# Moving the attention's transposes to the front of the full-array block in a windowed-attention and Fourier kernel

## The chip, the cores and the metric

The kernel runs on one core of one Trainium2 chip. The metric is the device time of one launch in microseconds (us); lower is better. The core has a matrix engine (PE, with its weight loads listed apart as PEld), a vector engine (DVE), a scalar engine (ACT), GpSimd (POOL) and a queue that only issues DMAs here (SP). All arithmetic is in float32.

## The reference, cut to what matters

The input is 32 images of 56 x 56 tokens with 128 channels. Two residual layers follow each other:

```
x = x + attention(groupnorm(x))      # 7x7 windows, shifted by 3, 4 heads of 32
x = x + ff(fourier(groupnorm(x)))    # DCT along each axis, 32 modes, mix, inverse DCT
                                     # ff: relu(h @ W1 + b1) @ W2 + b2, 512 hidden
```

Each group normalization is over 4 channels and the whole image, so an image's second layer starts only when all of its attention is done. The attention is `softmax(q k' + bias + mask) v`, then a projection with bias.

## The kernel before, in words

Nothing goes to another core and each image is loaded once. The attention works by rows of windows: an image has 8 rows (`NWR`) of 8 windows. One *cycle* starts one row; the loop at the end of the function runs over 8 x 32 cycles and a tail. In a cycle the PE does, for different rows and images, these pieces, which the text names by letters:

- **Q**: the products for queries and keys of row `cycle` (`attn_qk`, lines 363 and 370, one matmul each of 392 columns). ACT writes q (line 366) and half of k (line 375), DVE the other half of k (line 383).
- **S**: the scores of row `cycle` (`attn_scores`, line 417). DVE adds the bias (line 425). `attn_max` takes the maximum on DVE (435) and subtracts it on POOL (436). `attn_exp` is one ACT instruction (442). One cycle later `attn_divide` sums on DVE (447), takes the reciprocal (449) and multiplies on POOL (450).
- **W**: the values of row `cycle` (`attn_v`, line 395, ACT copy on line 402).
- **T**: the transposes of the finished attention matrix (`attn_transpose`, line 461, 8 matmuls; copies by DVE on 471 and ACT on 469).
- **V**: attention times values, row `cycle - 2` (`attn_values`, line 486, 64 small matmuls). ACT and DVE move the result to `oT` (lines 519, 517).
- **P**: the projection of that row (`attn_project`, line 528). DVE adds it to the image (536), SP writes the rows to `scr` in DRAM (542).
- **G**: two rows of the next image are transposed and copied to `xw` by ACT (`image_groups`, line 262; copies on 274, 275, 280; statistics on DVE, line 284). Its bias addition on POOL is `image_bias` (line 293). `image_norm` turns the statistics into scaled weights: a chain of small DVE instructions (lines 320 to 338), one POOL power (342), an ACT multiplication (349), `nb` on DVE (346) and a matmul N (line 352).
- The Fourier layer of earlier images: `transform` (637), `mix` (671; ACT copies `z`, SP writes `zscr`), `load_modes` (SP reads `zT`, line 692), `modes_back` **B** (710), `ff_in` **F** (753, 8 matmul records for one group of tokens, ACT relu on 761, POOL addition of `b2` on 743) and `ff_out` **O** (773, DVE addition on 785, SP output on 797 to 805).

The pieces use the array in different shapes: Q, T, P, G, F and O take all of it, W, `transform` and `mix` 128 x 64 of it, S and B 64 x 64, V 32-column tiles. A cycle runs through them in the order `full_first` (full array), `half_columns`, `quarters`, `eighths`, `full_last` (full array), so `full_last` and the next `full_first` form one block.

The order on PE, ACT, DVE and POOL is the order in which the program is written (`manual_schedule` names these four engines). The order of the DMAs on SP is left to the framework's own planner.

The Fourier work of the image in its *phase* c = (cycle - 10) mod 8 is spread by c: phase 0 `transform` along the width, 1 and 2 along the height, 3 `mix` (height), 4 and 5 `mix` (width), 4 to 7 B (two groups each). The feed-forward part is cut in 7 groups of tokens by `FF_GROUPS`; `FF_AT` says at which c, counted on to 14, each one runs. So a group runs in phases 7, 0, 1, 2, 4, 5 and 6, and phase 3 has none. G runs at the end of phases 1, 2, 3 and 4, the norm of the next image in phase 5. Cycles 0 to 9 (`first_rows`) have attention alone.

PSUM is cut in two pools of four banks that are handed out in turn: `pa` for the attention, `pc` for the Fourier layer. A matmul that takes a bank waits until the copy out of the bank's last use is done.

Of the kernel before, what the change touches and what calls it, by code (L numbers as in the profile page):

```python
# [23 lines left out]
WT = WS * WS  # L24
# [14 lines left out]
HALVES = (slice(0, P // 2), slice(P // 2, P))  # L39
SQRT_S = float(np.sqrt(float(S)))  # L40
QS = HD ** (-0.5)
FF_GROUPS = (HB, HB, HB, HB, HB, 320, 256)
FF_AT = (7, 8, 9, 10, 12, 13, 14)
PW = JP + WT
CONV_BEGIN = NWR + 2
# [3 lines left out]
def swin_fourier_kernel(  # L49
# [194 lines left out]
    def image_begin(b):  # L244
        im = Image()
        im.b = b
        im.x = xls.pop(b) if b in xls else load_image(b)
        im.xw = {}
        im.st = small.tile([P, NWR, 6], F32, tag="st0", name="st0", bufs=2)
        im.part = small.tile([TC, 2, C // 4, NWR], F32, tag="part", name="part", bufs=1)  # L250
        im.scr = dram.tile([S, S, C], F32, tag="scr", name="scr", bufs=2)
        return im

    def image_groups(im, i):


        pt = [attn_bank(), attn_bank()]
        pts = [
            p[:, : n * S].rearrange("p (j r s) -> p j r s", r=n, s=WS) for p, n in zip(pt, (8, 6))
        ]  # L260
        for c in range(7):
            nc.tensor.transpose(  # L262
                pts[c // 4][:, :, 2 * (c % 4) : 2 * (c % 4) + 2],
                im.x[:, WS * i // 2 + c],
                ident_x[:, :, SS:].rearrange("p r (j s) -> p j r s", s=WS),
            )
        for k in range(2):

            im.xw[i + k] = big.tile([P, RT + JP - WT], F32, tag="xw", name="xw", bufs=10)
            nc.gpsimd.memset(im.xw[i + k][:, RT:], 0.0)  # L270
            xw = im.xw[i + k][:, :RT]
            dst = xw.rearrange("p (j r s) -> p j r s", r=WS, s=WS)
            if k:
                nc.scalar.copy(dst[:, :, 0], pts[0][:, :, WS])
                nc.scalar.copy(
                    dst[:, :, 1:].rearrange("p j r s -> p j (r s)"),
                    pts[1].rearrange("p j r s -> p j (r s)"),
                )
            else:
                nc.scalar.copy(  # L280
                    dst.rearrange("p j r s -> p j (r s)"),
                    pts[0][:, :, :WS].rearrange("p j r s -> p j (r s)"),
                )
            nc.vector.bn_stats(im.st[:, i + k], xw)
        if im.b:
            image_bias(im, i)

    def image_bias(im, i):

        n0, n1 = WS * i // 2, WS * (i + 2) // 2  # L290
        for a, e in ((n0, n0 + 4), (n0 + 4, n1)):
            piece = im.x[:, a:e]
            nc.gpsimd.tensor_tensor(  # L293
                piece, piece, bproj.unsqueeze(1).to_broadcast([TC, e - a, C]), ALU.add
            )
# [158 lines left out]
    def attn_transpose(im, i, r):  # L454

        a = a_sb[r % 3]
        im.aT = []
        for hf in range(2):
            pt = attn_bank()
            for h in range(NH):  # L460
                nc.tensor.transpose(  # L461
                    pt[:PW, h * P : h * P + PW],
                    a[:PW, h, 2 * hf : 2 * hf + 2].rearrange("p w j -> p (w j)")[:, :PW],
                    ident[:PW, :PW],
                )
            aT = work.tile([P, 4, P], F32, tag="aT", name="aT")
            src = pt[:PW].rearrange("p (m x) -> p m x", x=P)[:, :, :PW]
            if hf:
                nc.scalar.copy(aT[:PW, :, :PW], src)  # L469
            else:  # L470
                nc.vector.tensor_copy(aT[:PW, :, :PW], src)
            im.aT.append(aT)

    def attn_values(im, i, r):


        v = v_sb[r % 3]
        po = [attn_bank(), attn_bank()]
        HALF = RT // 2
        po4 = [p[:, :HALF].rearrange("p (r n s) -> p n r s", r=WS, s=WS) for p in po]  # L480
        for f in range(2):
            for e in range(2):
                for h in range(NH):
                    for u in range(2):
                        ks = slice(u * JP, u * JP + WT)
                        nc.tensor.matmul(  # L486
                            po4[u][h * HD : (h + 1) * HD, 2 * f + e],
                            lhsT=v[ks, 2 * f + e, h * HD : (h + 1) * HD],
                            rhs=im.aT[f][ks, h, e * JP : e * JP + WT],
                            start=True,  # L490
                            stop=True,
                        )

        if i % 2 == 0:
            im.oT = work.tile([P, 2 * RT], F32, tag="oT", name="oT")
        oT = im.oT


        oTr = oT[:, i % 2 * RT : (i % 2 + 1) * RT].rearrange("p (r x) -> p r x", x=S)
        for u in range(2):  # L500
            src = po[u][:, :HALF].rearrange("p (r f x) -> p r f x", r=WS, f=2)
            x0 = SS + u * 2 * WS
            if not u:
                dst = bass.AP(
                    oTr.tensor, oTr[:, :, x0:].offset, [oTr.ap[0], [S, WS], [4 * WS, 2], [1, 2 * WS]]
                )
                parts = [(dst, src)]
            else:
                n = S - 4 * WS - x0
                parts = [  # L510
                    (oTr[:, :, x0 : x0 + 2 * WS], src[:, :, 0]),
                    (oTr[:, :, S - n : S], src[:, :, 1, :n]),
                    (oTr[:, :, 0:SS], src[:, :, 1, n:]),
                ]
            for d, f in parts:
                if u:
                    nc.vector.tensor_scalar(d, f, im.bias[:, 2:3], None, ALU.add)  # L517
                else:
                    nc.scalar.activation(d, f, AF.Identity, bias=im.bias[:, 2:3])
# [310 lines left out]
        return []  # L830

    def full_first(cycle, norm):
        im, i = row(cycle - 2)
        if im:
            attn_transpose(im, i, cycle - 2)
        last, j = row(cycle - 3)
        if last:
            sums = attn_sums(last, j)
            next(sums)
        im, i = row(cycle)  # L840
        if im:
            attn_qk(im, i, False)
        for im, c in fourier(cycle):
            for width, g in back_groups(c):
                load_modes(im, width, g)
        next(norm)
        if last:
            next(sums)
        for im, c in fourier(cycle):
            if c == 0:  # L850
                im.stats = fourier_stats(im)
                im.cols = {}
                next(im.stats)
                load_columns(im, 0)
                load_columns(im, 1)
        for im, c in fourier(cycle):
            if c in FF_AT:
                ff_in(im, FF_AT.index(c))
        for im, c in fourier(cycle):
            if c == 0:  # L860
                next(im.stats)
        if row(cycle - 1)[0]:
            attn_divide(cycle - 1)
# [29 lines left out]
    def eighths(cycle):  # L893
        im, i = row(cycle - 2)
        if im:
            attn_values(im, i, cycle - 2)

    def last_out(cycle):
        for im, c in fourier(cycle):
            if c in FF_AT:  # L900
                ff_out(im, FF_AT.index(c))

    def full_last(cycle, norm):
        next(norm)
        if row(cycle - 2)[0]:
            last_out(cycle)
        next_image(cycle)
        if row(cycle)[0]:
            attn_exp(cycle)
        im, j = row(cycle - 2)  # L910
        if im:
            attn_project(im, j)
        next(norm)

    def next_image(cycle):
# [9 lines left out]
    def first_rows(cycle, norm):  # L925
        im, i = row(cycle)
        if im:
            attn_qk(im, i, True)
        if cycle:
            attn_exp(cycle - 1)  # L930
        last, j = row(cycle - 3)
        if last:
            attn_project(last, j)
        im2, i2 = row(cycle - 2)
        if im2:
            attn_transpose(im2, i2, cycle - 2)
        if cycle:
            attn_divide(cycle - 1)
        if im:
            attn_scores(im, i, cycle)  # L940
            attn_max(cycle)
        if im2:
            attn_values(im2, i2, cycle - 2)
        next(norm)
        if last:
            for _ in attn_sums(last, j):
                pass
        if im:
            attn_v(im, i, cycle)
        if cycle < NWR // 2:  # L950
            image_bias(im, 2 * cycle)
        next(norm)
        next_image(cycle)
        if cycle == CONV_BEGIN - 1:
            attn_exp(cycle)
            attn_project(im2, i2)
        next(norm)

    def nothing():
# [100 lines left out]
```

## Time and profile before

| | |
|---|---|
| median of 4 runs | 3686.62 us (3685.34 to 3689.6) |
| the profiled execution, its own time | 3687.07 us |
| its span, first to last instruction | 3685.3 us |
| mean granted PE clock | 0.997 |
| PE busy | 3611.7 us, 61184 matmuls |
| DVE, ACT, POOL busy | 2213.6, 2144.9, 1372.5 us |
| DMA | 388.92 MB, mean 106 GB/s |

The rows of the timeline have the start in us from the span's beginning, the busy time, the engine, the line, what is written from what, and in brackets the idle time just before the instruction with what ended it. Matmuls overlap each other, so a block's length is best taken from its start to the start of the next block. The times of single steps below come from one image in the middle of the profiled execution, around 1560 to 1680 us; the other images repeat it.

### The profile page before, as it was taken

The numbers are of one execution on the slowest core, as the hardware profiler recorded it, in microseconds if no ns is written. First come the engines' busy times: TensorE is split into PE (matmuls) and PEld (weight loads), VectorE is DVE, ScalarE is ACT, GpSimd is POOL, SyncE is SP. The second block draws the span as 40 slices with busy tenths as digits, with TensorE's granted clock in tenths as the row PEclk, the third lists the DMA queues.
The fourth block names the chain that finished last, engine by engine and source line by source line (L and its number), as shares of the span: only waits on it lengthen the run. The fifth ranks groups of instructions, "written<-read, shape, count | busy, mean of one in ns | idle before, by whom it ended". The sixth has DMA issues, their size and how long they took to land.

```text
span 3685.3 us, 139865 instructions
## 1 busy us (share of the span) xinstructions
PE 3611.7 (98%) x61184; PEld 2940.1 (80%) x61184; DVE 2213.6 (60%) x4739; ACT 2144.9 (58%) x4043; POOL 1372.5 (37%) x1421
## 2 busy tenths in 40 slices
PE   7899999999999999999999999999999999999999
PEld 5687888888878888888788887878887888888777
DVE  7756566556665566665666665666656666656641
ACT  5565555655565655566555556555665565565553
POOL 5343334333333333343333343333343333433321
PEclk9999999999999999999999999999999999999999
DMA  4344443443433344334434344443344343433333
GB/s 115 97 106 109 105 110 91 119 106 104 113 96 107 107 110 109 104 96 112 110 101 114 97 110 107 106 113 96 104 107 113 102 114 96 112 107 104 96 102 96
DMA packets 687266, 388.92 MB, mean 106 GB/s; under 512 B 39967, under 2 KB 657600, under 8 KB 686400
## 3 DMA queue, kind: packets, MB, share of 16 engines
q1 hardware_dynamic: 686045, 379.65, 38.0%
q8 instruction: 482, 7.90, 0.9%
q14 instruction: 128, 1.05, 0.1%
q10 hardware_dynamic: 611, 0.32, 0.0%
HBM read 218.29 MB, written 161.48 MB: 103 GB/s over the span
## 4 chain that ended last, share of the span: by engine, by line
PE 91%; DMA 3%; DVE 3%; ACT 1%; issue 1%; POOL 0%; SPq 0%; POOLq 0%; DVEq 0%; ACTq 0%
PE pc L773 20%; PE pc L753 17%; PE pa L395 7%; PE pc L671 6%; PE pc L637 6%; PE pa L528 6%; PE pa L461 5%; PE pa L417 5%; PE pa L363 5%; PE pa L486 4%; PE pc L710 4%; PE pa L370 4%; DMA zT<-zscr 3%; PE pa L262 2%; DVE a L425 1%
## 5 line engine op out<-in xcount | busy, mean ns | idle before, releaser
L773 PE MATMUL pc<-wff,hid 128*128 128x128 f32 x6400 | 779.9, 279 | 1.0 <-ACT hid L761 0.9
L450 POOL TENSOR_TENSOR a<-a,rs 128x784 f32<-128x784 f32 x256 | 389.4, 1521 | 977.9 <-DVE rs L449 872.2
L773 PEld LDWEIGHTS pc<-wff,hid 128*128 128x128 f32 x6400 | 731.8, 190 | 23.5 <-issue 2.6
L753 PE MATMUL pc<-xf,wff 128*128 128x512 f32 (+2 forms) x1792 | 710.7, 539 | 0.9 <-DVE xf L721 0.7
L753 PEld LDWEIGHTS pc<-xf,wff 128*128 128x128 f32 x1792 | 339.3, 190 | 310.1 <-issue 228.8
L761 ACT ACTIVATE hid<-pc,b1sb 128x512 f32<-128x512 f32 (+2 forms) x896 | 532.7, 636 | 87.8 <-PE pc L753 84.0
L436 POOL TENSOR_TENSOR a<-a,mx 128x784 f32<-128x784 f32 x256 | 389.1, 1520 | 453.0 <-DVE mx L435 442.9
L785 DVE TENSOR_TENSOR res<-pc,res 128x512 f32<-128x512 f32 (+3 forms) x257 | 144.0, 571 | 615.1 <-issue 324.8
L293 POOL TENSOR_TENSOR xl<-xl,bproj 112x512 f32<-112x512 f32 (+1 forms) x256 | 286.3, 1141 | 376.1 <-PE pa L262 376.1
L425 DVE TENSOR_TENSOR a<-pa,bm 128x392 f32<-128x392 f32 x512 | 259.7, 550 | 193.4 <-PE pa L417 193.4
L442 ACT ACTIVATE a<-a 128x784 f32<-128x784 f32 x256 | 225.1, 879 | 210.3 <-POOL a L436 210.0
L383 DVE TENSOR_SCALAR k<-pa,heads,bqkv 128x392 f32<-128x392 f32 x246 | 168.5, 685 | 287.6 <-ACT k L375 287.6
L469 ACT COPY aT<-pa 113x452 f32<-113x452 f32 x256 | 137.0, 535 | 301.8 <-PE pa L461 296.8
L402 ACT COPY v<-pa 128x512 f32<-128x512 f32 x256 | 152.6, 596 | 271.0 <-PE pa L395 270.9
L517 DVE TENSOR_SCALAR oT<-pa,bqkv 128x98 f32<-128x98 f32 (+2 forms) x768 | 170.6, 277 | 226.0 <-PE pa L486 226.0
L743 POOL TENSOR_TENSOR res<-res,b2sb 128x512 f32<-128x512 f32 (+2 forms) x256 | 264.0, 1036 | 96.3 <-DMA res<-scr 96.3
L417 PEld LDWEIGHTS pa<-k,q 64*64 64x64 f32 x8192 | 183.5, 132 | 133.9 <-DVE rs L449 68.2
L395 PE MATMUL pa<-wn,xw 128*64 128x128 f32 x4096 | 281.9, 280 | 5.8 <-DVE a L425 3.4
L395 PEld LDWEIGHTS pa<-wn,xw 128*64 128x64 f32 x4096 | 219.8, 137 | 55.9 <-issue 16.4
L528 PE MATMUL pa<-wproj,oT 128*112 128x128 f32 x1792 | 244.2, 276 | 13.9 <-DVE oT L517 7.2
L280 ACT COPY xw<-pa 128x392 f32<-128x392 f32 x128 | 62.1, 485 | 325.9 <-PE pa L262 323.1
L435 DVE TENSOR_REDUCE mx<-a 128x16 f32<-128x784 f32 x256 | 247.1, 965 | 5.5
(91 smaller groups left out, 6071.2 us busy)
## 6 DMA issues: line engine op xcount, KB each, us to landing
zscr<-z SPq DMA_DIRECT2D x512, 112.0 KB
htok<-scr SPq DMA_DIRECT2D x256, 196.0 KB
zT<-zscr SPq DMA_DIRECT2D x192, 256.0 KB
res<-scr SPq DMA_DIRECT2D x160, 256.0 KB
out_dram<-res SPq DMA_DIRECT2D x160, 256.0 KB
scr<-xl SPq DMA_DIRECT2D x128, 224.0 KB
xl<-in_x_dram SPq DMA_DIRECT2D x32, 784.0 KB
xl<-in_x_dram SPq DMA_DIRECT2D x32, 672.0 KB
```

The lines of the kernel that those rows point to most:

```text
L293: nc.gpsimd.tensor_tensor(piece, piece, bproj.unsqueeze(1).to_broadcast([TC, e - a, C]), ALU.add)
L395: nc.tensor.matmul(pv[hs, j * C : (j + 1) * C], lhsT=im.xw[i][:, w * WT : w * WT + JP], rhs=im.w[:, 2 * C : 3 * C], start=True, stop=True,)
L417: nc.tensor.matmul(ps[hp][HALVES[e], pr * 2 * WT : (pr + 1) * 2 * WT], lhsT=q[cs, w * WT : w * WT + JP], rhs=k_sb[cs, :, w], start=True, s ...
L425: nc.vector.tensor_tensor(a[:, 2 * hp : 2 * hp + 2, :, 0:WT].rearrange("p u w j -> p w u j"), ps[hp][:, :RT].rearrange("p (w u j) -> p w u ...
L435: nc.vector.tensor_reduce(mx, a3, axis=AX.X, op=ALU.max)
L436: nc.gpsimd.tensor_tensor(a3, a3, mx.unsqueeze(2).to_broadcast([P, 2 * NWR, WT]), ALU.subtract)
L450: nc.gpsimd.tensor_tensor(a3, a3, rs.unsqueeze(2).to_broadcast([P, 2 * NWR, WT]), ALU.mult)
L528: nc.tensor.matmul(pp[:TC, (n - n0) * C : (n - n0 + 1) * C], lhsT=oT[:, (n - base) * TC : (n - base + 1) * TC], rhs=wproj, start=True, sto ...
L743: nc.gpsimd.tensor_tensor(res[:m, c0:c1], res[:m, c0:c1], b2sb[:m].unsqueeze(1).to_broadcast([m, c1 - c0, C]), ALU.add,)
L753: nc.tensor.matmul(ph[:, :n], lhsT=wff1[:, f * P : (f + 1) * P], rhs=xff[:, t0 : t0 + n], start=True, stop=True,)
L761: nc.scalar.activation(hf[:, :n], ph[:, :n], AF.Relu, bias=b1sb[:, f : f + 1])
L773: nc.tensor.matmul(pf[:m, c * C : (c + 1) * C], lhsT=im.hid[f][:, c * P : c * P + m], rhs=wff2[:, f], start=(f == 0), stop=(f == NF - 1),)
```

## The change

It has six parts.

1. T of a row moves from the start of `full_first` of one cycle to the start of `full_last` of the cycle before, ahead of O. The new function `transpose_next` issues it. Since two rows' transposes now exist at a time, `im.aT` becomes a dictionary by row.
2. In `full_last` P moves ahead of G and of the exponential. The order there was: norm step, O, G, exponential, P, norm step. It is now: T, norm step, O, P, G, exponential, norm step.
3. The seven groups of `FF_GROUPS` are reordered: the 320 and 256 tokens move from places six and seven to places five and six, and a group of 512 comes last. In phases: phase 4 has 320 instead of 512, phase 5 has 256 instead of 320, phase 6 has 512 instead of 256.
4. `image_bias` is merged into `image_groups`, so that image 0 gets its bias there too and not in cycles 0 to 3.
5. In `first_rows` the first step of the next image's norm moves from behind V to the place behind the exponential of the row before. It has an effect in cycle 7 alone.
6. At the end of cycle 9, T of row 8 is issued behind P, where `full_first` of cycle 10 issued it.

```diff
-FF_GROUPS = (HB, HB, HB, HB, HB, 320, 256)
+FF_GROUPS = (HB, HB, HB, HB, 320, 256, HB)
...
             nc.vector.bn_stats(im.st[:, i + k], xw)
-        if im.b:
-            image_bias(im, i)
-
-    def image_bias(im, i):
 
         n0, n1 = WS * i // 2, WS * (i + 2) // 2
...
     def full_first(cycle, norm):
-        im, i = row(cycle - 2)
-        if im:
-            attn_transpose(im, i, cycle - 2)
         last, j = row(cycle - 3)
...
+    def transpose_next(cycle):
+
+
+        im, i = row(cycle - 1)
+        if im:
+            attn_transpose(im, i, cycle - 1)
+
...
     def full_last(cycle, norm):
+        transpose_next(cycle)
         next(norm)
-        if row(cycle - 2)[0]:
+        im, j = row(cycle - 2)
+        if im:
             last_out(cycle)
+            attn_project(im, j)
         next_image(cycle)
         if row(cycle)[0]:
             attn_exp(cycle)
-        im, j = row(cycle - 2)
-        if im:
-            attn_project(im, j)
         next(norm)
...
         if cycle:
             attn_exp(cycle - 1)
+        next(norm)
         last, j = row(cycle - 3)
...
         if im2:
             attn_values(im2, i2, cycle - 2)
-        next(norm)
         if last:
...
-        if cycle < NWR // 2:
-            image_bias(im, 2 * cycle)
         next(norm)
         next_image(cycle)
         if cycle == CONV_BEGIN - 1:
             attn_exp(cycle)
             attn_project(im2, i2)
+            transpose_next(cycle)
         next(norm)
```

More of the change, by code (lines that the diff above doesn't have):

```diff
@@ L247, in image_begin @@
         im.x = xls.pop(b) if b in xls else load_image(b)
-        im.xw = {}
+        im.xw, im.aT = {}, {}
         im.st = small.tile([P, NWR, 6], F32, tag="st0", name="st0", bufs=2)
@@ L456, in attn_transpose @@
         a = a_sb[r % 3]
-        im.aT = []
+        im.aT[i] = []
         for hf in range(2):
@@ L471, in attn_transpose @@
                 nc.vector.tensor_copy(aT[:PW, :, :PW], src)
-            im.aT.append(aT)
+            im.aT[i].append(aT)
     def attn_values(im, i, r):
@@ L488, in attn_values @@
                             lhsT=v[ks, 2 * f + e, h * HD : (h + 1) * HD],
-                            rhs=im.aT[f][ks, h, e * JP : e * JP + WT],
+                            rhs=im.aT[i][f][ks, h, e * JP : e * JP + WT],
                             start=True,
```

## The prediction

> **What bounds the kernel now.** I read the page first, then the waits of PE, then the timeline of one image (1560 to 1680 us), which repeats every 112.8 us.
>
> ```profile
> PE 3611.7 (98%) x61184; PEld 2940.1 (80%) x61184; DVE 2213.6 (60%) x4739; ACT 2144.9 (58%) x4043; POOL 1372.5 (37%) x1421
> PE 91%; DMA 3%; DVE 3%; ACT 1%; issue 1%; POOL 0%; SPq 0%; POOLq 0%; DVEq 0%; ACTq 0%
> ```
>
> PE sets the end. No other engine is near full, so only what PE waits for, or executes more slowly, counts. The change removes no arithmetic. The waits of PE:
>
> ```profile
> PE pc L710 <- DMA zT<-zscr: 10.7, 24, 1.4
> PE pa L352 <- DVE nb L346: 9.3, 2, 4.7
> PE pa L528 <- DVE oT L517: 7.2, 5, 2.3
> PE pa L461 <- POOL a L450: 0.3, 1, 0.3
> ```
>
> They are small, and the modelled ends of matmuls hide some. I therefore took block lengths from start to start and compared equal blocks: over images 2 to 31 the excess above the shortest is 13.2 us at B of phase 6, 15.3 us at G of phase 3 (some 12 of it waiting for `oT`) and 6 us around N. That is what can be won, besides what a new order costs. The fourth line shows that T hardly ever waits for its matrix where it stands.
>
> Phase 3, the one without O:
>
> ```profile
> 1601.15 0.81 PE L486 MATMUL pa<-aT,v 49*32 49x49 f32 x64
> 1601.89 0.98 PE L262 MATMUL pa<-ident_x,xl 112*128 112x112 f32 x7
> 1602.21 0.66 DVE L517 TENSOR_SCALAR oT<-pa,bqkv 128x98 f32<-128x98 f32 x3
> 1603.02 1.10 PE L528 MATMUL pa<-wproj,oT 128*112 128x128 f32 x8
> 1605.44 0.87 ACT L442 ACTIVATE a<-a 128x784 f32<-128x784 f32 x1 [1.95 <-POOL a L436]
> ```
>
> G takes 1.13 us to P's start, against 0.72 elsewhere (1619.18 to 1619.89): P waits for `oT`, 0.15 us behind its DVE row's end. The exponential is here 3.5 us later than G.
>
> From phase 4 to 5:
>
> ```profile
> 1619.18 0.88 PE L262 MATMUL pa<-ident_x,xl 112*128 112x112 f32 x7
> 1619.79 0.48 ACT L280 COPY xw<-pa 128x392 f32<-128x392 f32 x1 [3.75 <-PE pa L262]
> 1620.60 0.89 ACT L442 ACTIVATE a<-a 128x784 f32<-128x784 f32 x1
> 1621.34 0.84 PE L363 MATMUL pa<-xw,wn 128*128 128x392 f32 x2
> 1623.65 0.69 DVE L383 TENSOR_SCALAR k<-pa,heads,bqkv 128x392 f32<-128x392 f32 x1 [0.85 <-ACT k L375]
> 1624.92 0.90 PE L417 MATMUL pa<-k,q 64*64 64x98 f32 x32
> 1628.49 1.52 POOL L450 TENSOR_TENSOR a<-a,rs 128x784 f32<-128x784 f32 x1
> 1629.67 0.81 PE L486 MATMUL pa<-aT,v 49*32 49x49 f32 x64
> ```
>
> ACT makes G's copies and the exponential before it can write q and k. P and T stand between G and Q and hide this. The division ends at 1630.01, only 0.40 us before V's end (1630.41), where T will stand.
>
> Phase 6:
>
> ```profile
> 1636.19 0.48 SPq L692 DMA_DIRECT2D zT<-zscr  x1
> 1636.81 1.89 PE L753 MATMUL pc<-xf,wff 128*128 128x256 f32 x8
> 1638.79 0.90 PE L417 MATMUL pa<-k,q 64*64 64x98 f32 x32
> 1640.77 1.00 PE L710 MATMUL pc<-idctw,zT 64*64 64x112 f32 x32 [0.31 <-DMA zT<-zscr]
> ```
>
> F of 256 tokens ends before k is written (S starts 0.06 us after DVE's k), and B's second half waits for a load issued 4.6 us earlier.
>
> **The change part by part**, per image in the steady state.
>
> *(a) T between V and O.* O's 32 matmuls take 3.68 us behind V (1655.40 to 1659.08) at 0.112 us each, 0.10 more than 32 of them. P's 8 take 0.93 behind the wait after G in phase 3, 0.87 behind O: 0.06 more. No block behind another full-array block shows such an extra. With T first I expect 0.06 there and nothing at O: 0.04 won in each of seven phases, 0.28 (bounds 0 and 0.7). The Trainium skill (TensorEngine Tiling (Array Packing), Key Properties) says that a change of the tiling mode drains the engine, whoever comes next; by that the switch is only moved, and the sum would be 8 us smaller. T's eight matmuls and two copies are otherwise the same, and T's banks are free: they were last used by S's second half and W, whose ACT copy ends at V's end in phase 6 (1643.42), 0.4 us before T's fifth matmul.
>
> *(b) Phase 3.* V 0.74 and T 0.86 reach 1602.75, P still starts at 1603.02, then P 0.93 and G 0.72 with Q at 1604.67, against 1604.74: 0.07 won. DVE's T copy runs behind the maximum, to 1604.30; G's second bank needs it at 1604.35. No gain from here is safe, but none is lost.
>
> *(c) Phase 4, 320 instead of 512.* F takes 2.25 instead of 3.53, so what waits behind it has 1.28 less cover. The exponential waits for POOL as before (1605.44); without T's copy, q starts at 1606.23 and DVE's k ends at 1608.10. S is due at 1608.25: free by 0.1. `zT` landed at 1607.8 and 1608.55 (issue at 1604.97 and 1605.40), needed at 1609.0 and 1609.8: covered. I take 0; bound 0.3.
>
> *(d) Phase 5, 256 instead of 320, Q directly behind G.* With Q's start as 0: G starts at -0.71, its first copy is 0.61 later, the exponential 1.42 later (0.71), q 0.78 behind that (1605.44 to 1606.22) at 1.49, k on ACT at 1.97, DVE's k 0.71 behind and done at 3.36, S possible at 3.42. PE gets there at 1.33 + 1.83 = 3.16: wait 0.26. V then ends at 3.42 + 0.73 + 1.26 + 0.92 + 1.85 + 0.74 = 8.92. The division ends 6.36 behind the start of DVE's k (1623.65 to 1630.01): 9.04, T at about 9.1. Lost: 0.26 + 0.15 = 0.41 (bounds 0.1 and 0.9). Queued behind T on PE are O, P and N; on ACT and DVE, T's copies stand before `wn` and `nb`, which N needs only 2.6 us later. In phases 2 and 3 the same ACT delay of 0.4 us is covered: S comes at Q + 4.9 and 5.9, T has 2.7 and 1.3 us to spare. T in phases 0, 1, 4, 6, 7: 1.2 us or more.
>
> *(e) Phase 6, 512 instead of 256.* S's wait goes: 1.98 against the 1.83 that 8 x 0.216 + 0.10 gives, 0.15. For B: behind P the path to B's second half gets 1.55 us longer by F and 0.9 shorter by T, and P itself comes 0.36 earlier after V. The load, issued behind P's write on SP, has some 0.7 us more; the wait was 13.2 / 29 = 0.45 a piece, 0.9 at most. Won: 0.6 (bounds 0.2 and 0.7). T behind N paid 0.11, Q behind N probably half: 0.07 won.
>
> Sum: -0.28 - 0.07 + 0 + 0.41 - 0.60 - 0.07 = -0.61 us an image, 30 times: **-18.3 us**.
>
> *(f) Once.* First image, where no O fills phases: W waited 0.65, 0.83, 0.62 and 0.78 us for a bank that T's late ACT copy held (now G's, copied first), and P waited 1.1 to 2.3 us behind V in three cycles, of which T fills 0.86 each: -5.5. Last image's phase 3: -0.9. Cycle 7's norm: its DVE chain (2.6 us) now runs ahead of the row's DVE work, but `nb` stays behind the sums in DVE's order; only DVE's idle 0.35 us goes: -0.4. PE's idle time there falls from 4.6 to some 2.3 us. After 4.6 us the 392-column matmuls ran at 0.80 instead of 0.43 us apart, 2.2 us lost in that cycle; after 2.90 us idle (at 103.67) the next blocks were slow too; after 1.06 us (113.81) not. I take no gain; bound -2.2. The Trainium skill (TensorE: Matmul & The Clock Gate, What's actually happening) puts the idle window at about 3.4 us; by that the 2.2 us would be won, though the 2.90 us row disagrees. Image 0's bias: four pairs of 2.24 us on POOL end near 17.3 us instead of inside cycles 0 to 3, where they delayed nothing; the power at 17.08 slips 0.3 us at most, hidden by the bias table, which lets the first scores through only at 27.5. Tail: phase 4's shorter F uncovers `zT` (it waited 0.46 already), and four output chunks instead of two end the kernel: +1.3. Together **-5.4 us** (bounds -10 and +2).
>
> From the profiled execution: 3687.07 - 18.3 - 5.4 = 3663.4. It lay 0.45 above the median: **3663**.
>
> **Rivals.** *Slower: ACT's exponential becomes the bound.* Moved between G's copies and Q, it is on the path to S in phases 4 and 5, exactly where F was shortened, and DVE's k delays the division for T. Against it: the rows above give 0 and 0.41. For it: margins of 0.1 us. Each 0.1 us that q, k and the division come later than computed costs up to 0.3 us an image (S in 4, S and T in 5), so the change turns at 0.25 us; at 0.4 us it is -23.7 + 36 = +12, 3699. *No change*: SP's order is the planner's. If the load in phase 6 stays as late as it is and (a) gives nothing, -0.61 + 0.45 + 0.28 = +0.12 us an image; 30 times that and -5.4 make -1.8, 3685. *More*: with k in time in phase 5 and 0.1 at each O, -0.61 - 0.41 - 0.42 = -1.44 us an image, 3638.
>
> **Numbers.** Forecast case 0.62 (its own range 3648 to 3678), more 0.05, no change 0.13, slower 0.20. The range runs from 3646 to 3697: some 0.05 below, 0.13 above. 0.2% or 7 us is what a measurement of this kernel can tell from no change: faster 0.67, same 0.13, slower 0.20.
>
> **What would show it.** Right: no DMA wait at B in phase 6, O at 3.58 us, W in cycles 11 to 14 without wait. Also S in phase 5 waiting some 0.3 us for DVE's k, and a POOL wait at T in phase 5. Wrong: S of phase 4 or 5 waiting a microsecond, `zT` late in phase 4, or O still 3.68 behind T.

## The result and the profile after

The kernel after takes 3682.87 us (median of 42 runs) where the kernel before takes 3687.66 (63 runs): a ratio of 0.9987 with the interval 0.9982 to 0.9991. That is 4.8 us, or 0.13%: inside what the prediction called no difference, and 20 us short of the forecast. The profiled execution took 3683.4 us with a span of 3681.6; the one before took 3687.07.

PE is busy for 3607.4 us, 98% of the span (3611.7 and 98% before). From the page, the chain that ended last:

```profile
PE 85%; DVE 5%; DMA 4%; ACT 2%; POOL 2%; issue 1%; SPq 1%; ACTq 0%; POOLq 0%; DVEq 0%
```

PE still sets the end, but its share of the chain fell from 91% to 85%, and DVE, POOL, DMA and ACT gained most of what it lost: more of the steps are now released by another engine. The waits of PE (engine, tile, line, what ended the wait: us in total, times, longest) say which:

```profile
PE pc L706 <- DMA zT<-zscr: 8.1, 19, 1.2
...
PE pa L413 <- DVE k L379: 7.3, 32, 0.8
...
PE pa L457 <- POOL a L446: 3.3, 3, 2.4
...
PE pa L524 <- DVE oT L513: 2.0, 2, 1.0
```

Lines are four lower than before. P's wait for `oT` (L524) fell from 7.2 to 2.0 us. B's wait for `zT` (L706) is still 8.1 of 10.7 us, S waits for DVE's half of k (L413) 32 times instead of once, and T now waits for the division (L446).

The modelled ends of matmuls hide part of such waits, so the accounts below go by block starts. I took the time from a block's start to the next one's, in the mean over images 2 to 31. An image took 112.92 us before and takes 112.84 now: 0.08 us less, where 0.61 was forecast. By phase:

| phase | before | after | what moved |
|---|---|---|---|
| 0 | 16.28 | 16.34 | "issue" stalls: transform 3.58 to 3.40, V 0.79 to 1.04 |
| 1, 2, 7 | 44.07 | 44.02 | T and O only |
| 3 | 10.44 | 10.34 | P no longer waits for `oT` behind G |
| 4 to 6 | 42.14 | 42.13 | next two views |

The three phases with the new group sizes are compared as a sum, since the same work stands in other phases. They stayed equal because two waits went and three came. Phase 4 (after, the timeline of all engines):

```profile
1602.91 0.38 SPq L688 DMA_DIRECT2D zT<-zscr  x1
...
1603.39 0.45 SPq L538 DMA_DIRECT2D scr<-xl  x1
...
1603.89 5.25 SPq L688 DMA_DIRECT2D zT<-zscr  x3
...
1606.67 2.04 PE L706 MATMUL pc<-idcth,zT 64*64 64x112 f32 x64
```

The same place before:

```profile
1604.97 0.93 SPq L692 DMA_DIRECT2D zT<-zscr  x2
1606.01 0.44 SPq L542 DMA_DIRECT2D scr<-xl  x1
```

SP now issues the write of the attention row (`scr<-xl`) between the two reads of `zT` that B of phase 4 needs. Before, both reads went out first (1604.97 and 1605.40). Both orders are the same in every image counted. Measured from the start of Q, the second read goes out at 1.52 us instead of 0.66, and its last packet lands at 5.20. F of 320 tokens lets B's second half get there at about the same time, so B takes 2.01 us in the mean instead of 1.64.

Phase 4 to 5 (after, the same view):

```profile
1617.29 0.48 ACT L280 COPY xw<-pa 128x392 f32<-128x392 f32 x1 [3.47 <-PE pa L262]
...
1618.10 0.89 ACT L438 ACTIVATE a<-a 128x784 f32<-128x784 f32 x1
...
1618.72 1.89 PE L749 MATMUL pc<-xf,wff 128*128 128x256 f32 x8
...
1620.07 0.69 DVE L379 TENSOR_SCALAR k<-pa,heads,bqkv 128x392 f32<-128x392 f32 x1 [0.77 <-ACT k L371]
...
1620.81 0.90 PE L413 MATMUL pa<-k,q 64*64 64x98 f32 x32 [0.20 <-DVE k L379]
...
1624.90 1.52 POOL L446 TENSOR_TENSOR a<-a,rs 128x784 f32<-128x784 f32 x1 [0.45 <-DVE rs L445]
...
1626.48 0.87 PEld L457 LDWEIGHTS pa<-ident,a 113*113 113x113 f32 x8 [0.24 <-POOL a L446]
```

ACT copies G, then runs the exponential, then writes q and k. DVE's half of k ends at 1620.76 and S starts 0.05 us later. At the end of the row the division ends at 1626.42 and T starts 0.06 later. F of 256 tokens takes 2.08 us to S's start instead of 1.83, V 0.92 instead of 0.74.

Phase 6 (after, the timeline of PE):

```profile
1635.83 1.71 PE L706 MATMUL pc<-idctw,zT 64*64 64x112 f32 x64
1637.47 1.09 PE L391 MATMUL pa<-wn,xw 128*64 128x128 f32 x16
...
1639.58 1.05 PE L457 MATMUL pa<-ident,a 113*113 113x113 f32 x8
1640.46 3.75 PE L769 MATMUL pc<-wff,hid 128*128 128x128 f32 x32
1644.05 0.82 PE L524 MATMUL pa<-wproj,oT 128*112 128x128 f32 x6
```

B runs through in 1.64 us: the wait for `zT` is gone here. And T to O to P: T takes 0.88 and O 3.59. Before, O behind V took 3.68 and T behind P 0.79. The sum is the same to 0.01 us.

### The profile page after: what moved, and what is told of

It reads as the page before. It is cut to its first block, busy times and chain, and to the rows that moved or that the text cites. A ratio compares the mean times of both kernels' runs of the same rounds, so it can differ in the third digit from the quotient of the medians.

```text
span 3681.6 us, 139841 instructions
## 1 busy us (share of the span) xinstructions
PE 3607.4 (98%) x61184; PEld 2941.7 (80%) x61184; DVE 2226.6 (60%) x4741; ACT 2126.3 (58%) x4043; POOL 1372.0 (37%) x1421
## 4 chain that ended last, share of the span: by engine, by line
PE 85%; DVE 5%; DMA 4%; ACT 2%; POOL 2%; issue 1%; SPq 1%; ACTq 0%; POOLq 0%; DVEq 0%
PE pc L769 19%; PE pc L749 16%; PE pa L457 6%; PE pa L391 6%; PE pc L633 6%; PE pa L524 5%; PE pa L413 4%; PE pa L359 4%; PE pa L482 4%; PE pa L366 4%; PE pc L667 4%; PE pc L706 3%; PE pa L262 2%; DMA zT<-zscr 2%; DMA zscr<-z 1%; POOL a L446 1%
## 5 line engine op out<-in xcount | busy, mean ns | idle before, releaser
L769 PE MATMUL pc<-wff,hid 128*128 128x128 f32 (+1 forms) x6400 | 760.6, 276 | 1.0 <-ACT hid L757 0.8
L769 PEld LDWEIGHTS pc<-wff,hid 128*128 128x128 f32 (+1 forms) x6400 | 732.4, 190 | 10.0 <-issue 2.9
L446 POOL TENSOR_TENSOR a<-a,rs 128x784 f32<-128x784 f32 x256 | 389.4, 1521 | 912.2 <-DVE rs L445 885.0
L362 ACT ACTIVATE q<-pa,bqkv 128x392 f32<-128x392 f32 x256 | 150.2, 587 | 285.4 <-PE pa L359 283.7
L739 POOL TENSOR_TENSOR res<-res,b2sb 128x512 f32<-128x512 f32 (+2 forms) x256 | 263.7, 1035 | 99.3 <-DMA res<-scr 99.3
L413 PEld LDWEIGHTS pa<-k,q 64*64 64x64 f32 x8192 | 183.4, 132 | 139.7 <-DVE rs L445 45.5
L457 PE MATMUL pa<-ident,a 113*113 113x113 f32 x2048 | 267.8, 274 | 7.8 <-POOL a L446 3.3
```

Of the source, the lines that this page charges most:

```text
L413: nc.tensor.matmul(ps[hp][HALVES[e], pr * 2 * WT : (pr + 1) * 2 * WT], lhsT=q[cs, w * WT : w * WT + JP], rhs=k_sb[cs, :, w], start=True, s ...
L446: nc.gpsimd.tensor_tensor(a3, a3, rs.unsqueeze(2).to_broadcast([P, 2 * NWR, WT]), ALU.mult)
L457: nc.tensor.transpose(pt[:PW, h * P : h * P + PW], a[:PW, h, 2 * hf : 2 * hf + 2].rearrange("p w j -> p (w j)")[:, :PW], ident[:PW, :PW],)
L739: nc.gpsimd.tensor_tensor(res[:m, c0:c1], res[:m, c0:c1], b2sb[:m].unsqueeze(1).to_broadcast([m, c1 - c0, C]), ALU.add,)
L769: nc.tensor.matmul(pf[:m, c * C : (c + 1) * C], lhsT=im.hid[f][:, c * P : c * P + m], rhs=wff2[:, f], start=(f == 0), stop=(f == NF - 1),)
```

## The experiments

**Theory.** Every part is good by itself or harmless, but two of them spend the same cover (work of PE that hides a wait). Moving P ahead of G makes ACT write q and k later, and makes SP send the row's write earlier. Shortening F in phases 4 and 5 takes away the time that would have hidden both. **Rival 1:** T ahead of O does win what was forecast, and something unrelated eats it. **Rival 2:** the new group order loses by itself. The ratios are to the kernel before, timed on the same chip; the period is that of one image in the profiled execution. Before it was 112.92, after 112.84.

| run | edit to the kernel after | ratio | interval | period, us |
|---|---|---|---|---|
| after | none | 0.9987 | 0.9982 to 0.9991 | 112.84 |
| e1_groups_back | old `FF_GROUPS` | 0.9935 | 0.9922 to 0.9947 | 112.34 |
| e2_groups_alone | before, with the new `FF_GROUPS` only | 0.9953 | 0.9941 to 0.9966 | 112.38 |
| e3_groups_early | 256 and 320 in phases 1 and 2 | 0.9905 | 0.9890 to 0.9920 | 111.85 |
| e4_g_before_p | G ahead of P again | 0.9924 | 0.9912 to 0.9937 | 112.21 |
| e5_read_first | phase 4's reads ahead of the row's write | 0.9954 | 0.9941 to 0.9966 | 112.57 |
| e6_exp_first | exponential ahead of G's copies | 0.9966 | 0.9954 to 0.9979 | 112.76 |
| e7_t_back | T back ahead of Q | 0.9995 | 0.9986 to 1.0004 | 113.08 |
| e8_early_and_g | e3 and e4 together | 0.9884 | 0.9870 to 0.9897 | 111.69 |
| e9_once_back | parts 4 and 5 undone | 0.9995 | 0.9986 to 1.0004 | 112.99 |
| e10_g_and_groups_back | e1 and e4 together | 0.9921 | 0.9908 to 0.9935 | 112.26 |

e9 has the steady state of the kernel after, instruction for instruction, and its period is 0.15 us longer. So periods of two profiles that lie 0.15 us apart, before and after among them, are not told apart by this; the lengths of single blocks repeat better.

### e1 and e2: the group order, with and without the rest

```diff
-FF_GROUPS = (HB, HB, HB, HB, 320, 256, HB)
+FF_GROUPS = (HB, HB, HB, HB, HB, 320, 256)
```

> The changed kernel with the old order of token groups (320 and 256 last). Theory of moved waits: the new order only moved the zT wait from phase 6 (0.45 us) to phase 4 (0.37 us) and made S and T wait in phase 5 (0.25 and 0.18 us). Undone: B of phase 4 at 1.64 again, F of phase 5 at 2.25 with no wait, V to T in phase 5 at most 0.1 us late, S of phase 6 0.15 us late again, B of phase 6 without wait because T no longer stands between P and Q and the loads come earlier on SP. Net -0.57 us an image, 17 us below the changed kernel, some 3666 us. Rival, something common to every order (the switch to T, code loading) pins the period: within 3 us of the changed kernel, 3680 to 3686.

e2 is the kernel before with the opposite edit and nothing else.

> The kernel before with the new order of token groups alone. Theory of moved waits: B of phase 6 and S of phase 6 lose 0.45 and 0.15 us; S of phase 5 does not wait, since P and T still stand between G and Q; S of phase 4 waits up to 0.2 us because the exponential there ends late; SP reads zT twice before the row's write, so B of phase 4 does not wait. Net -0.4 us an image, some 3676 us. Rival, the group order is itself worth nothing: 3685 to 3690.

The rest of the change without the new group order takes 0.65% off (period -0.58), the new group order without the rest 0.47% (-0.54). Together they bring 0.13% (-0.08). Rival 2 falls: the group order is good where the rest is missing. The two fall 1.04 us short of their sum, and not all of that is new waiting. Some 0.45 us is one wait counted twice: B of phase 6 takes 2.09 us before and 1.64 in e1 as in e2. In e2 the longer F covers its reads. In e1 F is as short as before, but SP issues both reads ahead of the outputs and the row's write, in most images over 1 us ahead of Q, where before they went out 0.2 us ahead of Q and 0.8 behind it. In e1, B of phase 4 takes 1.67 us, S of phase 5 doesn't wait (F of 320 in 2.25) and V there takes 0.76. In e2 all of phase 5 is free, and F of phase 4 takes 2.45, 0.2 for k: only there is the margin short already without the move.

### e3 and e4: give the cover back, or take the cause away

```diff
-FF_GROUPS = (HB, HB, HB, HB, 320, 256, HB)
+FF_GROUPS = (HB, HB, 256, 320, HB, HB, HB)
```

> The changed kernel with the groups of 256 and 320 in phases 1 and 2, and 512 in phases 4, 5 and 6. Theory of moved waits: phases 4, 5 and 6 all have the long F, so B of 4 and 6 find zT landed and S and T of 5 do not wait; in phase 1 no G precedes Q, so 256 is long enough for S (k done at Q + 3.0, S due at 3.16), in phase 2 320 is (3.42 against 3.58). Net -0.8 us an image against the changed kernel, some 3659 us. Rival, the waits follow the short groups wherever they go: 3675 to 3685.

```diff
             last_out(cycle)
-            attn_project(im, j)
         next_image(cycle)
         if row(cycle)[0]:
             attn_exp(cycle)
+        if im:
+            attn_project(im, j)
```

> The changed kernel with G ahead of P again (T stays in front of O, new group order). Theory that P ahead of G is what costs: P stands between G's copies and Q, so the exponential is hidden, S of phase 5 loses its 0.25 us and T of phase 5 its 0.18; SP reads zT twice before the row's write in phase 4, so B there loses most of its 0.37; in phase 3 G fills the wait for oT (0.2). Net -0.9 us an image, some 3657 us. Rival, only the group order costs and the place of P does not matter: 3678 to 3686.

e3 has the waits of phases 4, 5 and 6 all gone: phase 5's F, now of 512, in 3.53, V 0.74, B 1.67 and 1.64. The short groups stand in phases 1 and 2, where F takes 1.82 and 2.25 without a wait. e4 keeps the short groups where the change put them and removes the same waits from the other side: B of phase 4 1.69, F of phase 5 1.82, V 0.75. SP's order there is zT, zT, scr again. So either of the two, less exposed F or a later P, is enough. The gain of e4, 0.63 us, stayed under the 0.9 expected: its phase 0 takes 16.63 us, 0.29 more than in the kernel after, in stalls that the last section comes back to.

### e5: the order on SP alone

```diff
-            for width, g in back_groups(c):
-                load_modes(im, width, g)
+            if c != 4 or not row(cycle - 3)[0]:
+                for width, g in back_groups(c):
+                    load_modes(im, width, g)
...
             last_out(cycle)
+            for im1, c in fourier(cycle + 1):
+                if c == 4:
+                    for width, g in back_groups(c):
+                        load_modes(im1, width, g)
             attn_project(im, j)
```

> The kernel after, with one thing changed: the reads of zT for phase 4 are written in full_last of phase 3 ahead of P, so that P's write of the row stands behind both reads in SP's order, as in the kernel before. Theory (the planner put the row's write between the two reads of zT, and B of phase 4 waits for the second): B in phase 4 falls from 2.01 to about 1.65 us, the G behind it by up to 0.09, nothing else changes; 0.37 to 0.45 us an image, 30 times: 11 to 14 us less than the kernel after, 3671 us where the kernel before takes 3688 (ratio 0.9955). Rival (F of 320 tokens is simply too short for the load, whatever its place in the queue): B in phase 4 stays at 1.9 to 2.0, ratio 0.9985 as for the kernel after.

SP's own rows and PE's rows of e5 at the same place:

```profile
1602.57 0.93 SPq L688 DMA_DIRECT2D zT<-zscr  x2
1603.61 0.44 SPq L538 DMA_DIRECT2D scr<-xl  x1
```

```profile
1606.27 1.71 PE L706 MATMUL pc<-idcth,zT 64*64 64x112 f32 x64
1607.91 1.09 PE L391 MATMUL pa<-wn,xw 128*64 128x128 f32 x16
```

With both reads ahead of the write, B of phase 4 goes from 2.01 to 1.68 us (median 1.64) with F as short as in the kernel after. The rival is out: F of 320 tokens covers the loads, if the write doesn't stand between them. The kernel gained 0.33% on the kernel after (0.9954 against 0.9987), about 12 us. P to G in phase 4 stayed at 0.75 instead of 0.66; that 0.09 goes with the group of 320 tokens. Its O ends with matmuls on 64 of the array's columns (256 of them in the form 128*64 in the kernel's profile), so P behind it meets a change of the array's shape. P behind this O takes 0.09 to 0.10 more wherever the group stands: 0.96 instead of 0.87 in phase 5 before, 0.75 instead of 0.65 in phase 2 of e3.

### e6: the order on ACT alone

```diff
             attn_project(im, j)
+        early = (cycle - CONV_BEGIN) % NWR != 3
+        if early and row(cycle)[0]:
+            attn_exp(cycle)
         next_image(cycle)
-        if row(cycle)[0]:
+        if not early and row(cycle)[0]:
             attn_exp(cycle)
```

> The kernel after, with one thing changed: the exponential stands ahead of G's copies on ACT in all phases but 3, as it would if only P had moved. Theory (S in phase 5 waits 0.25 us for DVE's half of k and T 0.18 us for the division, because ACT makes G's two copies and the exponential one after the other before it can write q and k): both waits go, 0.43 us an image, 13 us less than the kernel after: ratio 0.995, with F of phase 5 at 1.83 instead of 2.08 and V at 0.74 instead of 0.92. B of phase 4 keeps its 2.0. Rival (the exponential itself waits for POOL's subtraction, so that G's copies come late instead, and Q behind them): F of phase 5 stays near 2.08 or G grows by the same 0.2 us; ratio 0.9985.

The rows of ACT in e6, phase 4 to 5:

```profile
1614.60 0.88 ACT L438 ACTIVATE a<-a 128x784 f32<-128x784 f32 x1
1618.18 0.49 ACT L280 COPY xw<-pa 128x392 f32<-128x392 f32 x1 [2.70 <-PE pa L262]
```

The exponential runs in ACT's idle time, 2.7 us before G's copies; nothing made it wait for POOL. S's wait is gone (F 1.82 instead of 2.08), and T's has fallen from 0.18 to 0.08 (V 0.82). Phase 5 won 0.36 us, as the theory has it but for 0.07. The ratio, 0.9966, is 8 us below the kernel after and 6 above the expectation: B of phase 4 rose by 0.08 to 2.09 and the "issue" stalls of phase 0 by 0.16 an image (e9, with the steady state of the kernel after, has 0.10 more there).

### e7: T alone

```diff
     def full_first(cycle, norm):
+        im, i = row(cycle - 2)
+        if im:
+            attn_transpose(im, i, cycle - 2)
...
     def full_last(cycle, norm):
-        transpose_next(cycle)
```

The call at the end of cycle 9 goes as well.

> The kernel after, with one thing changed: T is back at the start of full_first, ahead of Q, where the kernel before has it. Theory (the extra time at a change of the array's shape is paid by whichever block comes first, so T ahead of O wins nothing by itself): O goes back to 3.68 and T to 0.79 us, sum unchanged; the waits of S and T in phase 5 go (0.43 us won), P in phase 3 waits for oT directly behind V (0.3 to 0.8 us lost), B of phase 4 keeps its 2.0: ratio 0.997 to 1.001. Rival (T ahead of O does win the forecast's 0.28 us an image, and something else ate it): O back to 3.68 with T at 0.70, 8 us more than the above: ratio 0.999 to 1.003.

The rows of PE in e7, phase 3 and later phase 6 to 7:

```profile
1609.88 1.10 PE L524 MATMUL pa<-wproj,oT 128*112 128x128 f32 x8 [1.06 <-DVE oT L513]
...
1648.53 3.84 PE L769 MATMUL pc<-wff,hid 128*128 128x128 f32 x32
1652.21 0.82 PE L524 MATMUL pa<-wproj,oT 128*112 128x128 f32 x6
1652.86 0.96 PE L457 MATMUL pa<-ident,a 113*113 113x113 f32 x8
```

O takes 3.67 behind V and T 0.79 behind P: 4.46 together, against 4.47 with T first. Rival 1 falls: moving T to the front of the block wins nothing at the change of the array's shape. Phase 3 pays 0.94 us (11.28 against 10.34), since P now stands directly behind V and waits for `oT`, and phases 4 and 5 get 0.35 and 0.33 back, since T again stands between G and Q. B of phase 4 fell to 1.65, which I had not expected: with T ahead of Q SP issues the row's write first and the second read 0.42 us behind Q's start in the mean, against 1.39 in the kernel after. The ratio alone fits both expectations; the sum of T and O is what decides. With P ahead of G, what T's move is worth is the cover it gives to P in phase 3.

### e8 and e10: do the cures add up?

e8 is e3's and e4's edits together, e10 e1's and e4's.

> The kernel after with two of the earlier edits together: G stands ahead of P again, and the groups of 256 and 320 tokens run in phases 1 and 2, so that phases 4, 5 and 6 have 512 each. Theory (the moved work is good everywhere except where F was shortened or a load was passed on SP): the two edits mend partly the same waits, so they do not add up; what is left over the kernel with early groups alone is G behind V in place of P in phase 3 (0.1 us an image): ratio 0.989 to 0.990, near 3652 us where the kernel before takes 3690. Rival (they mend different waits and add up): ratio 0.985, 3634 us.

> The kernel after, with G ahead of P again and the old order of the groups, so that of the steady state only T's move is left. Theory (P ahead of G is what makes the new group order cost time; without it the group order hardly matters): the period is that of the kernel with the old groups alone, 112.34, less 0.07 us in phase 3: about 112.25, the same as with G ahead of P and the new groups (112.21); ratio 0.992 to 0.9935. Rival (G ahead of P is worth its 0.63 us an image whatever the groups): period 111.7, ratio 0.987 to 0.988.

They don't add up: e8 lies 0.21% below e3, not 0.63%, and the rival's 0.985 is outside its interval. With G ahead of P the group order is worth nothing either way (112.21 new, 112.26 old), while behind P ahead of G it cost 0.50. So P ahead of G and the short groups in phases 4 and 5 are one cause, not two. In e10 T's move alone brings 0.66 us an image, most of it at B of phase 6 (2.09 to 1.64, by SP's earlier reads as in e1), so the new groups find that wait gone. e8 is the fastest version run, 3648.91 us where the kernel before took 3692.09 on that chip.

### e9: the parts that act once

```diff
+        if im.b:
+            image_bias(im, i)
+
+    def image_bias(im, i):
...
             attn_exp(cycle - 1)
-        next(norm)
...
             attn_values(im2, i2, cycle - 2)
+        next(norm)
...
+        if cycle < NWR // 2:
+            image_bias(im, 2 * cycle)
```

> The kernel after, with parts 4 and 5 of the change undone: image 0 gets its bias in cycles 0 to 3 and the first step of the norm stands behind V in cycle 7, as before. Theory (these two parts change only when the first ten rows start, by less than the 3.4 us by which the same rows differ between profiled executions): ratio 0.998 to 0.9995, the period of an image stays at 112.8, the first Q starts near 18.4 us instead of 20.7 and cycle 7 takes 11.5 instead of 11.1 to 11.35 us. Rival (the bias additions ahead of the power delay everything behind them by the 2.3 us): Q of row 18 starts at 188.7 and the ratio is 0.998 or lower.

The first Q starts at 18.1 instead of 20.7 us and cycle 7 takes 11.54 instead of 11.13, as expected, but row 18 starts at 193.3 (191.0 after): the rival's 188.7 is out. The ratio, 0.9995, overlaps the one of the kernel after, so whether these parts are worth 0 or 3 us is open. Three profiles without parts 4 and 5 (before, e2, e9) start row 10 at 99.3 to 100.9 us; nine with them at 97.6 to 102.3, 100.0 in the mean. No gain and no loss shows there.

## Why the prediction was wrong

Right, and to 0.1 us: **(b)**, phase 3 won 0.10 (0.07 forecast). **(d)**, S 0.25 and T 0.18 late in phase 5, 0.43 (0.41 forecast), by the chain that the prediction followed. e6 shortens that chain on ACT alone and takes away S's wait and more than half of T's with F as short as it was; e3 does it with a longer F, so the waits need both. **(e)**, B of phase 6 won 0.41 and S 0.15, and with the smaller pieces there some 0.68. The number is right, but for B partly by luck: the step let the longer F outweigh a path made shorter by T's move, and e1 and e10 show that T's move frees this B without any longer F, because SP then issues the reads earlier. N's surroundings won 0.11 where 0.07 stood: Q behind N pays nothing of what T behind N paid.

Three steps failed.

**Term (a): T between V and O, -0.28 an image, measured 0.00.** The step read O's extra 0.10 us as something that O pays, since P paid less in its place and no block behind another full-array block seemed to show it. It is paid by the first full-array block behind V, whichever it is: T took over 0.09 of it (0.79 to 0.88) and O lost 0.09. This is the sum that the prediction gave for the rule of the Trainium skill (TensorEngine Tiling (Array Packing), Key Properties), that a change of the tiling mode drains the engine; e7's 4.46 against 4.47 agrees with it. The price that the step put on T, 0.06, came from P in phase 3, which stood behind G, a full-array block, and behind a wait; no row of before had T directly behind V. A row of before did show the price: P behind the O of 320 tokens, which ends on 64 columns, took 0.96 instead of 0.87. 8 us of the miss.

**Term (c): phase 4, "covered: I take 0; bound 0.3", measured +0.37 at B.** (P to G takes 0.09 more there too, but P ahead of N takes 0.09 less in phase 5: that price moved with the group of 320.) The step took the issue times of `zT` from the trace before (1604.97 and 1605.40) and checked them against a shorter F. But the program moves P, and with it the row's write, which before stood behind both reads. The prediction knew that SP's order is the planner's, and used this for phase 6 alone. e5 puts the write back behind the reads and B is free. 11 us of the miss. Its own list of what would show it wrong named this ("`zT` late in phase 4").

**Term (f): -5.4 once, measured -1.3 in this pair.** (The spans of the two profiles differ by 3.7 us, and 30 times the 0.08 of the period makes 2.4 of it.) W's waits for banks went, as computed. But T waited for the division in phase 5 of the first image (2.4 us, the longest of the three in the third line of the waits above), and in the next 3.4 us the clock was at half: T and P took 1.66 and 1.71 us instead of 0.88 and 0.87. The pair also differs in the clock. Over rows 10 to 17 it was at half for 6.8 us in the profile before and for 13.6 in the one after. e7, the kernel after with T put back, had it at half for 13.7 us too and took 95.9 us for these rows, where the kernel after took 92.4. At 6.8 us T's old place has 92.7 (before) against 90.7 and 91.8 (e3, e6), at 17.1 us 96.4 (e2) against 94.0 and 94.2 (e8, e10). So T's move is worth some 1.5 to 3.5 us there, part of the 5.5; of these kernels only e7 and the kernel after differ by T alone. The gain that the prediction left as a bound for cycle 7, a clock that stays fast (-2.2), came in two profiles of the nine that have part 5: row 8 takes 6.73 us in e4 and e6 and 8.0 to 8.8 in the rest, 8.56 before.

The first two make 0.65 us an image, 19.5 us of the 20 that were missed, and the last 4; the gains above forecast in (e), at N and in (b), less the 0.02 of (d), gave 4 back. The rivals were each half right. "No change" had the time, to 2 us, with (a) as it came, but with the late load in phase 6; the load was late in phase 4, so the time was partly luck. "Slower" had ACT's exponential as the mechanism, which (d) priced correctly.

## What to carry to other kernels

A block that moves takes its DMAs along: before trusting a load's issue time from the old trace, list what the queue's planner may now put ahead of it. Two edits that each win can take away the same wait, and they can spend the same cover. So price them as a pair, above all at the place where one shortens the cover and the other lengthens the path (here 0.54 and 0.58 us an image alone, 0.08 together). An extra time at a change of the array's shape belongs to the place in the order, not to the instruction that shows it.

## What the runs showed of the hardware

**The clock after the same idle time.** In every one of the twelve profiles PE is idle 2.90 us before the statistics' matmul of row 10. In nine of them W and the transform behind it ran slowly, in three at full speed. The rows of PE, after and e4:

```profile
103.03 0.66 PE L575 MATMUL pa<-tot,gmean 112*128 112x64 f32 x2 [2.90 <-DVE tot L566]
103.62 1.98 PE L391 MATMUL pa<-wn,xw 128*64 128x128 f32 x16
```

```profile
101.96 0.41 PE L575 MATMUL pa<-tot,gmean 112*128 112x64 f32 x2 [2.90 <-DVE tot L566]
102.29 1.09 PE L391 MATMUL pa<-wn,xw 128*64 128x128 f32 x16
```

The granted clock over 100 to 110 us was 0.66 in the first and 1.00 in the second; row 10 took 15.31 and 12.44 us. The same holds for row 8, behind the norm: Q's start lies 0.75 us ahead of the next block's in two profiles and up to 1.45 ahead in the others. Row 18 starts between 188.8 and 197.6 us in the twelve profiles, more of a difference than the whole change made, and the clock behind these two gaps is up to 5 us of it (2.9 in row 10, 2.0 in row 8). The Trainium skill (TensorE: Matmul & The Clock Gate, What's actually happening) says that the activity window runs freely and does not begin with the kernel; a result that changes from run to run behind one idle time agrees with that. Its 3.4 us of idle time as the bound does not agree: 2.90 was enough in nine profiles.

The clock records in the twelve traces show what decides here. Within one profile the clock changes only at points that lie whole multiples of 3.41 us apart, and these points lie differently in each profile. In the nine, a stretch between two such points holds 2.04 to 2.90 us of idle time of PE, and the clock drops at its end. In the three, a point falls near the middle of the gap, and no stretch holds more than 1.73. No fixed bound follows: elsewhere in these profiles the clock dropped behind a stretch with 0.97 us (by the modelled ends of the matmuls) and stayed behind one with 1.96.

**"Issue" stalls go to where the order puts them.** PE waits, released by nothing that the profile shows, in the transform of phase 0 with T in the old place (3.58 us and V 0.79) and in V with T moved (3.40 and 1.04). Over the kernels with T moved, phase 0 takes 16.18 to 16.63 us in the mean, though its own instructions are the same. 0.45 us an image is 14 us over the kernel, as much as one of the edits is worth, and no run here says what sets it.
